# Moving part of a decoder layer's dense expert ahead of the routed experts, and its choice sums to other engines

## The chip, the cores and the metric

One core of a Trainium2 chip (trn2) runs the whole kernel in one launch. The metric is the device time of one execution in microseconds (us); lower is better. The engines of the core are TensorE (PE, with its weight loads as PEld), VectorE (DVE), ScalarE (ACT), GpSimd (POOL) and SyncE (SP)[...].

## The reference, cut to what matters

The kernel computes one decoder layer on x of 16 x 64 tokens by 256 columns, all in float32. Self-attention and cross-attention come first and are not touched. The last third is a mixture of experts on the normalized rows:

```python
scores = softmax(xt @ Wg.T)                # 1024 tokens, 16 experts
masked = scores where the expert's group is among the best 2 of 4 groups
topi = top_k(masked, 4)                    # 4 choices of each token
combine[t, topi] += scores[t, topi]
h = silu(xt @ W1[e].T) * (xt @ W3[e].T)    # each expert: 256 -> 176
y = sum over e of combine[:, e] * (h @ W2[e].T)
z = (silu(xt @ Ws1.T) * (xt @ Ws3.T)) @ Ws2.T     # shared expert, 352 wide
x = x + y + z
```

## The kernel before, in words

**Layout.** The 1024 tokens are 8 tiles of 128 rows, `x[0]` to `x[7]`; tiles 0 to 3 are half 0, 4 to 7 are half 1. A float32 product is made of two rounded parts, a high and a low one: ACT makes the high part (L112), DVE the low one (L113), and `three` (L107) multiplies high by high, high by low and low by high.

**The experts.** Experts 0 to 14 are computed on the rows that chose them only ("routed"). Expert 15, `w_last`, is computed densely, on all rows, and added with its weight, which is zero where it was not chosen (`add_last`, L933). The shared expert is dense too.

**Slots.** `choose` (L734) finds the four choices of each row and a place for each among 384 slots per expert. `send` (L820) writes rows to their slots in DRAM (`xd`) with indirect DMAs issued by POOL, four tiles for each choice and half. Of routed expert e, `expert_inputs` (L1233) loads the 384 rows on SP's queue once the sends of its possible choices have landed (expert 0 waits for first choices only, expert 1 for first and second, and so on), PE turns them (L1247), ACT and DVE make the parts `xs`. `expert_weights` loads 640 KB; ACT and DVE, later ACT, DVE and POOL, make the parts (L270, L275). `expert_hidden` (L1255) multiplies up (18 matmuls of 384 columns, `mm<-xs,w`) and gates. `send_outputs` (L1273) multiplies down (15 matmuls, `av<-w,hp`), copies to `y` (L1281) and writes the rows to the row's place in a second DRAM array, `yd`, with three indirect DMAs on POOL (L1286). `load_outputs(k)` (L1296) loads all choices number k back in four DMAs of 256 KB from SP's queue into `got` (nine buffers of two tiles for sixteen uses) once every send issued so far has landed. `add_outputs` (L1309) adds them with their weights `cw` (made by `weights_of_choices`, L852, one call for each half): for tiles 2 and 5 ACT scales (L1313) and POOL adds (L1314), for the other six one DVE instruction does both (L1316).

**Order.** The loop of L1335 runs over e: inputs of e, weights of e, hidden of e-1, outputs of e-2. For e = 2 alone, hidden of expert 1 is written ahead of the inputs of expert 2, and `issue_after(up_done[0])` puts the turning of expert 2's rows behind expert 1's up products on PE. A planner (`schedule_with_timeline_sim`, L1494) lays out each engine's queue: program order is the priority, and an instruction that its model takes to be ready may pass one that is not. `issue_after(ins)` only fixes an order on the engine of `ins`. On the chip each queue is then worked off in order, and an instruction that waits holds all behind it.

**Dense expert.** Half 0 is done ahead of the loop, beside the shared expert: `dense_up(0)` (L1069) with 512 columns at a time, `dense_gated`, `dense_out` (L1098). Half 1 is done in the last experts, 256 columns at a time: its first part's hidden at e = 16 (L1353), its output at L1368, its second part at L1370, between the additions of choices 0, 1 and of 2, 3.

**End.** L1364 puts the additions behind the last expert's instructions on each engine; each `x[i]` is then stored by SP or ACT's queue (L1374). An `If` (L1385) for slots that did not suffice ends the kernel; it is not entered here.

Of the kernel before, what the change touches and what calls it, by code (L numbers as in the profile page):

```python
# [35 lines left out]
NI = NT // 128  # L36
# [6 lines left out]
E, INTER, NGRP, TOPK, TOPKG = 16, 176, 4, 4, 2  # L43
# [28 lines left out]
def decoder_layer(ctx: ExitStack, tc: tile.TileContext, a: dict, out: bass.AP):  # L72
# [80 lines left out]
    norms, scaled, turned, silus, exps, softened = [], [], [], [], [], []  # L153
# [152 lines left out]
    with ExitStack() as attn:  # L306
# [545 lines left out]
        def weights_of_choices(half):  # L852


            shape = [128, 4, E]
            lg = logits[half]
            m = fs.tile([128, 4], F32, tag="r_m", name="r_m")
            nc.vector.tensor_reduce(m, lg, AX.X, ALU.max)
            p = fs.tile(shape, F32, tag=f"r_p{half}", name=f"r_p{half}")
            nc.vector.tensor_tensor(p, lg, m.unsqueeze(2).broadcast_to(shape), ALU.subtract)  # L860
            exps.append(nc.scalar.activation(p, p, AF.Exp).ins)
            s = fs.tile([128, 4], F32, tag="r_s", name="r_s")
            nc.vector.tensor_reduce(s, p, AX.X, ALU.add)
            nc.vector.reciprocal(s, s)
            nc.vector.tensor_tensor(p, p, s.unsqueeze(2).broadcast_to(shape), ALU.mult)
            sel = selected[half]
            last = fs.tile([128, 4], F32, tag=f"cl{half}", name=f"cl{half}")
            nc.vector.tensor_tensor(last, sel[:, :, E - 1], p[:, :, E - 1], ALU.mult)
            nth = fs.tile(shape, F32, tag="slot", name="nth_back")
            nc.vector.tensor_tensor(  # L870
                nth, places[half], sel[:, :, E - 1 :].broadcast_to(shape), ALU.add
            )
            ch = choices(nth, sel)
            kept = fs.tile(shape, F32, tag="slot", name="kept")
            nc.vector.scalar_tensor_tensor(kept, over[half], 0.5, p, ALU.is_lt, ALU.mult)
            nc.vector.tensor_tensor(
                ch, ch, kept.unsqueeze(1).broadcast_to([128, TOPK, 4, E]), ALU.mult
            )
            w = fs.tile([128, TOPK, 4], F32, tag=f"cw{half}", name=f"cw{half}")
            nc.vector.tensor_reduce(w, ch, AX.X, ALU.add)  # L880
            return w, last, p
# [57 lines left out]
        routed = []  # L939


        with (
# [143 lines left out]
            def dense_gated(g, up, g2, up2):  # L1086
                h_p = [
                    xa.tile([128, 512], F32R, tag=f"roped1{n}", name=f"dense1{n}", bufs=1)
                    for n in range(2)
                ]  # L1090
                h_p.append(xa.tile([128, 512], F32R, tag="q_r", name="dense2"))
                nc.vector.tensor_tensor(g, up, g, ALU.mult)
                parts_of(g, h_p[0], h_p[1])
                nc.vector.tensor_tensor(g2[:64], up2[64:], g2[64:], ALU.mult)
                parts_of(g2[:64], h_p[2][:64], h_p[2][64:])
                return h_p

            def dense_out(h_p, half, tiles, add):  # L1098
                for k in tiles:
                    ps = av_tile()[:, :D]  # L1100
                    expert_output(ps, w_last, h_p, slice(k * 128, k * 128 + 128))
                    add(half, k, ps)
# [9 lines left out]
            for n in range(len(units) + 2):  # L1112
# [58 lines left out]
                if n == 8:  # L1171
                    w_last = dense_weights()
                    with after(exps[-1]):
                        routed.append(weights_of_choices(0))
                if n == 9:
                    rows[1] = [
                        xw.tile([128, 3, 2, 2, DC], F32, tag="w_s", name="rows1")
                        .rearrange("p a b c d -> p (a b c d)")[:, : 2 * ROW]
                        .rearrange("p (a b) -> p a b", a=2)
                        for _ in range(2)  # L1180
                    ]
                    normed[1] = layernorm_t(3, (1,), token_rows(1))[0]
                    high = highs[-1]
                    scored, placed, aimed = choose(1)
                    sh = [
                        xb.tile([128, 2, 2, 4 * HQ], F32R, tag=f"w_q{m}", name=f"sh{m}")
                        .rearrange("p a b c -> p (a b c)")
                        for m in range(2)
                    ]
                    hs = []  # L1190
                    for k in range(3):
                        with after(*pn_turned[(0 if k else 1) :]):
                            up = shared_up(0, k, xa)
                            part = [t[:, k * 512 : (k + 1) * 512] for t in sh]
                            hs.append(shared_hidden(k, *up, xa, part))
                    send(0, (2,), [lows[-1]])
                    with after(projected, scaled[-1]):
                        shared_output(0, hs)
                    send(0, (3,), [high])
                    send(1)  # L1200
                    with after(high):
                        dense_ups = dense_up(0, turned[-1], scored, scored)
                    with after(aimed, scored):
                        ups = [shared_up(1, 0, xa)]
                    with after(aimed, placed):
                        ups.append(shared_up(1, 1, xa))
                        hs = [shared_hidden(k, *ups[k], xa) for k in range(2)]
                        ups.append(shared_up(1, 2, xa))
                        hs.append(shared_hidden(2, *ups[2], xa))
                        h_p = dense_gated(*dense_ups)  # L1210
                        shared_output(1, hs)
                        dense_out(h_p, 0, range(4), add_last)


    fw = ctx.enter_context(tc.tile_pool(name="fw", bufs=2, reuse_waits="tile"))
# [4 lines left out]
    gated, up_done = [None], [None]  # L1220
# [85 lines left out]
            tiles.append(t)  # L1306
        return tiles

    def add_outputs(k, got, cw):  # L1309
        for i in range(NI):  # L1310
            y, w = got[i // 2][:, i % 2], cw[i // 4][:, k, i % 4 : i % 4 + 1]
            if i % 3 == 2:
                nc.scalar.activation(y, y, AF.Copy, scale=w)  # L1313
                nc.gpsimd.tensor_tensor(x[i], x[i], y, ALU.add)  # L1314
            else:
                nc.vector.scalar_tensor_tensor(x[i], y, w, x[i], ALU.mult, ALU.add)  # L1316

    def dense_hidden(w, half, n):
        return expert_hidden(w, [p[:, :, n * 256 : n * 256 + 256] for p in normed[half]], 256)

    def dense_output(w, h_p, half, n, add):
        for b in range(2):
            ps = av_tile()[:, :D]
            expert_output(ps, w, h_p, slice(b * 128, b * 128 + 128))
            add(half, 2 * n + b, ps)
# [7 lines left out]
    with tc.issue_after(lows[-1]), tc.issue_after(silus[-1]):  # L1333
        ws[0] = expert_weights(a["W123"][0], nc.vector)
    for e in range(E + 1):  # L1335
        if e == 2:

            low = lows[-1]
            hs[e - 1] = expert_hidden(ws[e - 1], xs[e - 1][0], SLOTS)
        if e < E - 1:  # L1340
            low = lows[-1]
            with tc.issue_after(up_done[0] if e == 2 else low):
                xs[e] = expert_inputs(e)
            if e >= 1:
                with tc.issue_after(low), tc.issue_after(silus[-1]):
                    ws[e] = expert_weights(a["W123"][e], nc.vector if e < 3 else nc.gpsimd)
        if 0 <= e - 1 < E - 1 and e != 2:
            hs[e - 1] = expert_hidden(ws[e - 1], xs[e - 1][0], SLOTS)
        if e - 2 >= 0:
            if e == E:  # L1350

                with tc.issue_after(gated[0]):
                    h_p = dense_hidden(w_last, 1, 0)  # L1353
            last = send_outputs(e - 2, ws.pop(e - 2), hs.pop(e - 2), xs.pop(e - 2)[1])
            if e - 2 == E - TOPK - 2:
                short = slots_are_short()
            if e == 6:
                with tc.issue_after(gated[0]), tc.issue_after(silus[-1]):
                    routed.append(weights_of_choices(1))
            k = e - 2 - (E - 1 - TOPK)  # L1360
            if k >= 0:
                got[k] = load_outputs(k)
    with ExitStack() as behind_last:
        for ins in (*last, gated[0]):  # L1364
            behind_last.enter_context(tc.issue_after(ins))
        cw = [r[0] for r in routed]
        add_outputs(0, got[0], cw)
        dense_output(w_last, h_p, 1, 0, add_last)  # L1368
        add_outputs(1, got[1], cw)
        dense_output(w_last, dense_hidden(w_last, 1, 1), 1, 1, add_last)  # L1370
        for k in range(2, TOPK):
            add_outputs(k, got[k], cw)
    for i in range(NI):
        (nc.sync if i % 2 == 0 else nc.scalar).dma_start(  # L1374
            out=out[i * 128 : (i + 1) * 128, :], in_=x[i]
# [122 lines left out]
```

## Time and profile before

| | us |
|---|---|
| median of 3 runs (lowest, highest) | 592.65 (592.43, 593.28) |
| profiled execution, own time | 594.01 |
| its span, first to last instruction | 592.2 |

| engine | busy us | share of the span |
|---|---|---|
| PE | 558.4 | 94% |
| DVE | 403.4 | 68% |
| ACT | 280.6 | 47% |
| POOL | 232.5 | 39% |

Three stretches of the trace concern the change. From 446 to 460 us the shared expert's and the dense expert's first half run on PE while POOL sends rows; from 460 to 475 the first two routed experts start; from 560 to 592 the last experts end, and the choices are loaded, added and stored. The mean granted clock of PE over the span is 0.973 of full speed. A row of the timeline has the start, the duration of the merged instructions, engine, line, operation, written and read tile, shape and number of instructions, then the idle time ahead of it and what ended that. A busy time of merged matmuls is their stretch; a mean duration of one (300 to 400 ns) is longer than its share of that stretch (190 ns), since matmuls overlap.

### The profile page before, as it was taken

To read this page: it belongs to the slowest core of one execution; us is meant where nothing else is said; L and a number is where in the kernel's file an instruction comes from. 1 tells how busy PE (TensorE), PEld (TensorE's weight loads), DVE (VectorE), ACT (ScalarE), POOL (GpSimd) and SP (SyncE) were. 2 spreads that over 40 slices of the span, in tenths; PEclk is the share of its full clock that TensorE was granted. 3 is DMA by queue.
4 is the path that set the end of the run, shared out by engine and by line. 5 is a ranking of instruction groups with operands and counts; after the bars stand their busy time and mean duration, and the time that the engine had idled before them with its cause. 6 is when DMAs were issued, how large, how long until landed. Compare 5 with 4: busy or idle time off the path is not lost.

```text
span 592.2 us, 10572 instructions
## 1 busy us (share of the span) xinstructions
PE 558.4 (94%) x3999; PEld 452.9 (76%) x3999; DVE 403.4 (68%) x879; ACT 280.6 (47%) x524; POOL 232.5 (39%) x213
## 2 busy tenths in 40 slices
PE   5989999999999989999999999999989799999992
PEld 5878988988889875757777577576778688888871
DVE  5454636554465789847668487789648587888766
ACT  3657574575665432221431332333435276867551
POOL 4192000010000004526334454442545546768773
PEclk8989999999999999999999999999989799999996
DMA  8667042141300499481020000000413677565275
GB/s 247 159 195 208 25 136 91 53 143 50 95 1 1 137 265 293 128 243 30 1 70 1 8 1 1 28 2 26 165 69 95 231 225 239 176 228 184 100 252 184
DMA packets 56293, 70.82 MB, mean 120 GB/s; under 512 B 13872, under 2 KB 42768, under 8 KB 56240
## 3 DMA queue, kind: packets, MB, share of 16 engines
q1 hardware_dynamic: 51408, 58.71, 33.5%
q0 software_dynamic: 3696, 10.36, 4.6%
q10 hardware_dynamic: 1136, 1.05, 0.5%
q8 instruction: 32, 0.52, 0.4%
q14 instruction: 21, 0.17, 0.1%
HBM read 48.61 MB, written 21.86 MB: 119 GB/s over the span
## 4 chain that ended last, share of the span: by engine, by line


## 5 line engine op out<-in xcount | busy, mean ns | idle before, releaser
L973 POOL TENSOR_TENSOR roped<-rt,rt 128x512 f32<-128x512 f32 x48 | 62.7, 1328 | 82.8 <-DVE rt L967 80.5
L967 DVE TENSOR_TENSOR rt<-mm,rope_q 128x512 f32<-128x512 f32 x96 | 61.5, 684 | 23.7 <-PE mm L104 23.1
L104 PE MATMUL mm<-xn,w_q 128*128 128x512 f32 x288 | 74.2, 403 | 0.5 <-ACT xn L214 0.5
L104 PEld LDWEIGHTS mm<-xn,w_q 128*128 128x128 f32 x288 | 52.1, 188 | 14.4 <-issue 2.7
L1286 POOL DMA_INDIRECT yd<-y,to x45 | 49.4, 1099 | 34.7 <-DVE y L1281 13.5
L104 PE MATMUL mm<-xs,w 128*128 128x384 f32 x270 | 57.0, 358 | 1.2 <-ACT w L270 0.6
L104 PEld LDWEIGHTS mm<-xs,w 128*128 128x128 f32 x270 | 48.0, 196 | 4.4 <-DVE w L275 0.8
L318 ACT ACTIVATE p<-p 128x512 f32<-128x512 f32 x32 | 20.2, 630 | 65.7 <-DVE p L317 65.7
L513 POOL TENSOR_TENSOR wo<-code,scale 128x512 fp32r<-128x512 f32 x8 | 10.6, 1330 | 102.1 <-PE mm L104 94.1
L988 PE MATMUL mm<-roped,w_s 128*64 128x512 f32 x192 | 46.3, 601 | 0.0
L104 PE MATMUL av<-w,hp 128*128 128x256 f32 (+1 forms) x225 | 45.8, 314 | 0.1
L605 DVE TENSOR_TENSOR x<-mm,x 128x256 f32<-128x256 f32 x64 | 26.0, 419 | 29.1 <-PE mm L104 27.9
L104 PEld LDWEIGHTS av<-w,hp 128*128 128x128 f32 (+1 forms) x225 | 33.9, 187 | 9.0 <-issue 0.7
L104 PE MATMUL mm<-wo,o 128*128 128x256 f32 x256 | 39.5, 295 | 0.1
L104 PE MATMUL mm<-wv,xn 128*128 128x256 f32 x256 | 36.0, 292 | 1.4 <-ACT kT L550 1.4
L315 DVE TENSOR_REDUCE sm_m<-at 128x8 f32<-128x512 f32 x32 | 21.7, 679 | 21.8 <-PE at L565 20.9
L104 PE MATMUL mm<-xn,wq 128*128 128x512 f32 x128 | 35.4, 413 | 0.4 <-ACT xn L214 0.4
L104 PE MATMUL mm<-xn,wk 128*128 128x512 f32 x128 | 35.4, 407 | 0.0
L582 PE MATMUL av<-pt,v 128*128 128x128 f32 x256 | 34.5, 277 | 0.0
L104 PEld LDWEIGHTS mm<-wv,xn 128*128 128x128 f32 x256 | 32.5, 193 | 2.5 <-ACT kT L550 1.6
L104 PEld LDWEIGHTS mm<-wo,o 128*128 128x128 f32 x256 | 32.9, 190 | 1.5 <-issue 0.4
L582 PEld LDWEIGHTS av<-pt,v 128*128 128x128 f32 x256 | 32.0, 191 | 1.2
(216 smaller groups left out, 1150.1 us busy)
## 6 DMA issues: line engine op xcount, KB each, us to landing
w<-in_W SPq DMA_DIRECT2D x15, 640.0 KB
code<-in_codes SPq DMA_DIRECT2D x32, 256.0 KB
scale<-in_scales SPq DMA_DIRECT2D x32, 256.0 KB
xr<-xd SPq DMA_DIRECT2D x15, 408.0 KB
xd<-zeros SPq DMA_DIRECT2D x8, 720.0 KB
yd<-zeros SPq DMA_DIRECT2D x8, 512.0 KB
got<-yd SPq DMA_DIRECT2D x16, 256.0 KB
wq<-in_Wq SPq DMA_DIRECT2D x4, 512.0 KB
```

Source lines behind the costliest of these rows:

```text
L104: m = nc.tensor.matmul(ps, lhsT=l, rhs=r, start=(n == 0), stop=(n == len(pairs) - 1))
L315: nc.vector.tensor_reduce(m, sc, AX.X, ALU.max)
L318: exps.append(nc.scalar.activation(p, p, AF.Exp, scale=scale).ins)
L513: mults[n] = eng.tensor_tensor(w, *loaded[gr].pop(n), ALU.mult).ins
L582: nc.tensor.matmul(av[:, k * 128 : (k + 1) * 128], lhsT=v[:, i, k0 : k0 + HD], rhs=pt[:, i].rearrange("p a q -> p (a q)"), start=True, sto ...
L605: nc.vector.tensor_tensor(x[i], ps, x[i], ALU.add)
L967: nc.vector.tensor_tensor(mt, ps3, rope_table(t, 2 * ab + k), ALU.mult)
L973: nc.gpsimd.tensor_tensor(r.rearrange("p (b s) -> p b s", s=S), one, two, op)
L988: nc.tensor.matmul(ps[h // 2][(h % 2) * 64 : (h % 2) * 64 + 64], lhsT=w_s[:, t, blk, ab, :], rhs=roped[2 * t + ab], start=first[h], stop=l ...
L1286: sent = nc.gpsimd.indirect_dma_start(out=yd[: (E - 1) * SLOTS + min(TOPK, E - 1 - e) * NT], out_offset=bass.IndirectOffsetOnAxis(ap=to[:, ...
```

## The change

Three edits.

1. For e = 1 as well as e = 2, hidden of expert e-1 is written ahead of the inputs of e, and expert 1's turning goes behind expert 0's up products on PE. Since `silus[-1]` is then expert 0's, the parts of expert 1's weights go behind expert 0's gate on ACT.
2. The dense expert's half 1 leaves the last experts and is done whole ahead of the loop, 512 columns at a time, after half 0's output; the weights of the choices of half 1 are made there too, no longer at e = 6.
3. Choice 0 is added wholly by ACT (scale) and POOL (add), in three portions in iterations e = 14, 15 and 16, each written behind that iteration's three sends of rows and ahead of the next load of choices. Choices 1 to 3 are added at the end, tiles 1, 4 and 7 by ACT and POOL, five tiles by DVE.

```diff
                         dense_out(h_p, 0, range(4), add_last)
+                        routed.append(weights_of_choices(1))
+                        h_p = dense_gated(*dense_up(1, placed, placed, placed))
+                        dense_out(h_p, 1, range(4), add_last)
...
-    def add_outputs(k, got, cw):
-        for i in range(NI):
-            y, w = got[i // 2][:, i % 2], cw[i // 4][:, k, i % 4 : i % 4 + 1]
-            if i % 3 == 2:
+    def add_outputs(k, got, tiles=range(NI), others=(1, 4, 7)):
+        for i in tiles:
+            y, w = got[i // 2][:, i % 2], routed[i // 4][0][:, k, i % 4 : i % 4 + 1]
+            if i in others:
                 nc.scalar.activation(y, y, AF.Copy, scale=w)
                 nc.gpsimd.tensor_tensor(x[i], x[i], y, ALU.add)
...
-        if e == 2:
+        if e in (1, 2):
             low = lows[-1]
             hs[e - 1] = expert_hidden(ws[e - 1], xs[e - 1][0], SLOTS)
         if e < E - 1:
             low = lows[-1]
-            with tc.issue_after(up_done[0] if e == 2 else low):
+            with tc.issue_after(up_done[0] if e in (1, 2) else low):
                 xs[e] = expert_inputs(e)
...
-        if 0 <= e - 1 < E - 1 and e != 2:
+        if 0 <= e - 1 < E - 1 and e > 2:
             hs[e - 1] = expert_hidden(ws[e - 1], xs[e - 1][0], SLOTS)
         if e - 2 >= 0:
-            if e == E:
-                with tc.issue_after(gated[0]):
-                    h_p = dense_hidden(w_last, 1, 0)
             last = send_outputs(e - 2, ws.pop(e - 2), hs.pop(e - 2), xs.pop(e - 2)[1])
...
-            if e == 6:
-                with tc.issue_after(gated[0]), tc.issue_after(silus[-1]):
-                    routed.append(weights_of_choices(1))
             k = e - 2 - (E - 1 - TOPK)
+            if k >= 1:
+                tiles = ((), (0, 1, 2), (3, 4, 5), (6, 7))[k]
+                add_outputs(0, got[0], tiles, tiles)
             if k >= 0:
                 got[k] = load_outputs(k)
...
-        cw = [r[0] for r in routed]
-        add_outputs(0, got[0], cw)
-        dense_output(w_last, h_p, 1, 0, add_last)
-        add_outputs(1, got[1], cw)
-        dense_output(w_last, dense_hidden(w_last, 1, 1), 1, 1, add_last)
-        for k in range(2, TOPK):
-            add_outputs(k, got[k], cw)
+        for k in range(1, TOPK):
+            add_outputs(k, got[k])
```

## The prediction, made before the changed kernel was run

> **What bounds the kernel now.** I read the busy times by stretch first, to see which engine rules where the change works.
>
> ```profile
> 446.00:460.00 14.00, 14.00 (x84) 11.55 (x84) 11.51 (x23) 7.49 (x12) 9.51 (x9) 1.00 0.33 100
> 460.00:475.00 15.00, 10.67 (x49) 10.05 (x48) 7.63 (x17) 4.74 (x10) 8.08 (x8) 0.77 0.71 232
> 475.00:560.00 85.00, 83.89 (x485) 72.59 (x484) 70.58 (x131) 59.51 (x118) 57.39 (x48) 1.00 0.61 198
> 560.00:572.00 12.00, 12.00 (x72) 10.20 (x71) 7.08 (x13) 5.63 (x15) 8.52 (x8) 1.00 0.56 187
> 572.00:592.00 20.00, 7.71 (x39) 5.61 (x38) 15.01 (x31) 5.26 (x13) 9.52 (x11) 0.72 0.66 218
> ```
>
> The columns are stretch, length, busy PE, PEld, DVE, ACT, POOL, then PE's clock. PE is the bound in every stretch but 460 to 475, where it idles and its clock falls to 0.77, and the last 20 us, where DVE is busy 15. So a moved PE instruction costs its full time unless it falls into one of these two.
>
> Next, the timeline of PE where the routed experts start: expert 0's up products have begun, then PE stands still for expert 1's rows, with 15 of expert 0's 18 products queued behind the turning.
>
> ```profile
> 459.57 0.82 PE L1247 MATMUL at<-ident,xr 128*128 128x128 f32 x6
> 460.63 0.79 PE L104 MATMUL mm<-xs,w 128*128 128x384 f32 x3 [0.24 <-ACT xs L112]
> 465.50 0.87 PE L1247 MATMUL at<-ident,xr 128*128 128x128 f32 x3 [4.09 <-DMA xr<-xd]
> 466.03 3.23 PE L104 MATMUL mm<-xs,w 128*128 128x384 f32 x9
> 469.05 0.84 PE L1247 MATMUL at<-ident,xr 128*128 128x128 f32 x3
> 469.55 5.32 PE L104 MATMUL mm<-xs,w 128*128 128x384 f32 x24
> ```
>
> The gap is 4.09 us, and nine matmuls after it take 3.23 us, 0.36 each, where 18 take 3.41 later (0.19 each, at 540.13).
>
> Last, the end, as DVE and POOL see it.
>
> ```profile
> 571.47 5.00 DVE L1316 SCALAR_TENSOR_TENSOR x<-got,cw,x 128x256 f32<-128x256 f32 x10
> ...
> 585.54 1.66 DVE L1316 SCALAR_TENSOR_TENSOR x<-got,cw,x 128x256 f32<-128x256 f32 x4
> ```
>
> ```profile
> 561.98 1.11 POOL L1286 DMA_INDIRECT yd<-y,to  x1 [0.16 <-issue]
> ...
> 572.58 1.00 POOL L1286 DMA_INDIRECT yd<-y,to  x1 [0.30 <-ACT y L1281]
> 573.88 1.28 POOL L1286 DMA_INDIRECT yd<-y,to  x1 [0.30 <-ACT got L1313]
> 575.18 2.74 POOL L1314 TENSOR_TENSOR x<-x,got 128x256 f32<-128x256 f32 x3
> 578.98 2.46 POOL L1314 TENSOR_TENSOR x<-x,got 128x256 f32<-128x256 f32 x3 [1.06 <-ACT got L1313]
> 583.12 1.83 POOL L1314 TENSOR_TENSOR x<-x,got 128x256 f32<-128x256 f32 x2 [1.67 <-ACT got L1313]
> ```
>
> DVE works from 571.47 to 587.2 without a gap that the timeline marks: 24 additions (12.6 us) and the dense half's own gating and adding. It sets the end; the last store closes the span 5.0 us later. POOL issues its nine last sends one after the other from 561.98 to 575.16 and has only eight additions.
>
> [...] 0.36 us a matmul for 3.2 us after the gap, then 0.22, then 0.19. [...] POOL's additions take 725 to 1002 ns (median 902) beside a full DVE, while the same shape took 740 in the median at L634. [...] the send ending at 453.17 lets SP's load go at 455.20.
>
> **The change, step by step: the start.** Moving half 1 ahead adds PE work before the routed experts: 18 up products of 512 columns at 0.243 us (24 took 5.82 from 445.80), 4.4 us, and 20 down products at 0.191 (20 took 3.83 from 568.33), 3.8 us: +8.2. What they can hide in: the gaps of 4.09 and 0.24, which close because PE has work until about 468 while expert 1's rows land at 465.5: -4.3. Without the gap the clock stays up: from 465.50 to 474.87 PE does 33 up products and 6 turnings in 9.4 us, which at 0.189 and 0.137 would be 7.1: -2.3. Balance +1.6. Edit 1 closes the same gap, so it is worth nothing beside edit 2 (alone it would fill 15 x 0.19 = 2.9 us of it); what it costs is a wait: the ACT part of expert 1's weights (1.26) now stands behind expert 0's gate, with DVE's low part (0.95) behind that and expert 1's products behind both. Dense half 1's down products, 3.8 us, are there to cover its 2.2.
>
> New stalls: unknown. DVE gets from the move 2 gate products, 2 low parts (0.69 each), 4 additions (0.48) and the choices' weights (some 3.1 for thirteen small ones): 7.8 us on top of the 9.7 that it has from 450.94 until expert 0's rows are done. That is 17.6, filled until 468.5 at best, against PE's 468: no bound, but no slack. ACT gets 3.5 of gating and casts and two table loads (1.28 each). Between 0, if the planner's order always finds PE something ready, and 3.0, if the two chains take turns; a gain is excluded, as only idle PE time counted above can be won. The nearest row is half 0's own down products, 16 in 3.43 (0.214 against 0.191), 0.4 us lost. I take 1.0 for both products and weights.
>
> The weights of half 1's choices leave e = 6, where the table loads held ACT and PE waited 0.58 us for expert weights (at 512.32): -0.6. POOL's sends of rows and SP's loads keep their order there. So the routed experts run **2.0 us later** (1.6 + 1.0 - 0.6).
>
> **The end, in the clock of before.** PE loses 18 of the dense products (2.57 us of 561.19 and 566.80) between the last experts, so the last down product could end 2.3 to 2.6 us before 572.1; DVE goes from 24 additions to 15 and has nothing dense: some 8 us of work. What is next is POOL. From 561.98 on (it makes the last expert's low weights until 561.82, gated by ACT's cast, which PE does not advance) it has nine sends at 1.27 us from start to start (0.96 and 0.30 of issue), 11.4, and now 8 + 3 x 3 = 17 additions instead of 8. Their price: 0.725 at the least, 0.95 beside a full DVE; DVE is some 40% busy there, and I take 0.82: 13.9. With 0.4 for hand-overs POOL ends at 561.98 + 11.4 + 13.9 + 0.4 = **587.7**, against DVE's 587.2 before. The order among them does not matter: with the additions ahead, the last send ends at about 578.4, the last rows' load starts 2.4 later and is in by 586.4 (four loads, 5.6 us, estimated from got's second-last set: issue 574.30, second load in at 578.34), and the last scale and addition end at 588; with the sends ahead, 13 to 14 additions still follow 576. ACT's scales are covered by POOL's. In both the stores take the same 5.0 us. The end costs **+0.5**.
>
> Sum: 592.2 + 2.0 + 0.5 = 594.7 of span, and as the median lies 0.45 above that span, 592.65 + 2.5 = **595.1**. (The profiled execution itself took 594.01, 1.8 above its span; I carry only the difference over.)
>
> **Rivals.**
> - *The early stretch hides the moved half (not slower).* Place: PE from 446 to 475. PE is called full there, but down products at 0.214 and the stall behind DVE's additions show slack; if dense half 1 fills these too and brings no new stall, +2.0 becomes +0.2, giving 593.3; it decides once new stalls are under 0.4 us. Against it: DVE's 17.6 us.
> - *POOL is not the last.* Additions at 0.725 (-1.6), and the last store alone in the DMA queues in 4.0 instead of 5.0 us: 592.5. For it: DVE is relieved. [...] With the first rival also true, 590.7.
> - *In-order queues wait on each other (slower).* ACT's scale of choice 0 sits among the last expert's gates and waits for a DMA, POOL's addition waits for ACT, and sends stand behind it; and the two early chains take turns (3.0): +2.0 and +2.2 at the end, 599.3.
> - *The edit of the order does nothing of its own*: the time is the forecast's, since the gap is counted once.
>
> **How the numbers follow.** Forecast, 0.48, own range 593.9 to 597.2 (stalls 0 to 2, additions 0.78 to 0.88). First rival 0.16, second 0.11, both together 0.10, queues 0.15. About 1.2 us (0.2%) is what this kernel's measurement can tell. Below 591.4: both rivals together and part of each, 0.21. From 591.4 to 593.9: the rest of these, 0.2. Above: 0.59. The range runs from 590.5 (both first rivals, rounded down) to 599.3 (the queues' case; stalls of 3.0 and additions at 0.95, +2.0 and +2.2, give the same), which leaves out about 0.1 at the lower end and 0.06 at the upper.
>
> **What would show it.** PE has no gap over 1 us from 446 to 476 and its clock stays at 1.0; expert 1's up products end at 477.5; POOL is busy from expert 12's sends to within 1 us of the last addition; DVE idles in the last 15 us. Wrong if the last additions are DVE's, if POOL idles over 3 us there, or if the experts start no later than before.

## The result and the profile after

| | before | after |
|---|---|---|
| median (lowest, highest), us | 592.96 (592.43, 595.69), 4 runs | 613.37 (611.10, 614.44), 4 runs |
| ratio (95% interval) | | 1.033 (1.0286 to 1.0373) |
| profiled execution, own time and span | 594.01, 592.2 | 611.10, 609.0 |

The change makes the kernel 3.3% slower. The sign of the forecast was right; the size was not: 613.4 lies far above the range that ended at 599.3. The profiled execution is the fastest of the four, so the traces account for 16.8 us of the 20.4 between the medians. (Of the last two kernels of the table below 7 of 14 and 8 of 22 executions are slow, over 602 us, at a mean granted clock of 0.961 to 0.971 where the others have 0.969 to 0.985, against 1 of 35 of before beside them; they are in the median and left out of the ratio, and what slows them is not shown.)

To say where they went I cut each trace at two matmuls whose place no edit changes: the last of `placed` (L781), just ahead of the work that the change touches, and the one of `slots_are_short` (L838), when the outputs of expert 10 have been sent. What lies ahead of the first mark is the same program in every kernel here, yet its end falls anywhere from 441.7 to 450.0 us, so only stretches are compared, not clock times. Each stretch is of one profiled execution. Where kernels have the same program in a stretch, they differ by up to 1.5 us (117.6 to 119.1 in four of the table below, 40.7 to 42.1 at the end of six), so less than that is not read as an effect.

| stretch | before | after | difference |
|---|---|---|---|
| start to L781 | 445.6 | 442.8 | -2.8 |
| L781 to L838 | 105.8 | 119.0 | **+13.2** |
| L838 to the end | 40.8 | 47.2 | **+6.4** |

So the routed experts run 13.2 us later where 2.0 was forecast, and the end costs 6.4 where 0.5 was forecast.

First the busy times of after by stretch, with the columns of the prediction's first block (stretch, length, then busy PE, PEld, DVE, ACT, POOL, PE's clock, DMA share, GB/s).

```profile
457.00:472.00 15.00, 10.75 (x38) 7.42 (x36) 7.03 (x13) 5.83 (x8) 7.58 (x8) 0.80 0.53 182
...
590.00:609.00 19.00, 0.00 (x0) 0.00 (x0) 7.75 (x10) 3.05 (x6) 7.28 (x10) 0.50 0.53 171
```

The first row should have been full: in before a hole of 4 us stood there, for rows from DRAM, and the moved products were to fill it. It is as empty as before (10.75 busy of 15), and its clock is low (0.80). The last 19 us have no PE work at all.

The timeline of PE in after, where dense half 1 now stands:

```profile
456.69 4.46 PE L104 MATMUL mm<-xn,w_last 128*128 128x512 f32 x18
463.13 1.30 PE L104 MATMUL av<-w_last,dense 128*128 128x256 f32 x6 [1.97 <-ACT dense L112]
466.66 5.43 PE L104 MATMUL av<-w_last,dense 128*128 128x256 f32 x14 [2.22 <-DVE dense L113]
472.02 1.54 PE L1250 MATMUL at<-ident,xr 128*128 128x128 f32 x6
473.49 4.64 PE L104 MATMUL mm<-xs,w 128*128 128x384 f32 x18
...
480.42 0.79 PE L104 MATMUL mm<-xs,w 128*128 128x384 f32 x3 [1.64 <-ACT xs L112]
...
482.23 1.84 PE L104 MATMUL mm<-xs,w 128*128 128x384 f32 x9 [0.54 <-DVE xs L113]
```

The planner has put the shared expert and half 0 first, and the whole of half 1 after them. Between its up products and its down products PE's queue holds nothing else, so PE stands still while ACT and DVE make the gate: 1.97 us, six matmuls, 2.22 us. The 14 that follow take 5.43 us, 0.39 each against 0.19. From 456.69 to expert 0's turning at 472.02 half 1 has taken **15.3 us**; its products alone are the 8.2 of the prediction. ACT's side of that chain shows what it is made of:

```profile
458.44 1.28 ACT L1080 ACT_TABLE_LOAD   x1 [6.40 <-PE mm L104]
...
462.46 0.62 ACT L112 CAST dense<-dense 128x512 fp32r<-128x512 f32 x1
462.98 1.26 ACT L270 CAST w<-w 128x1280 fp32r<-128x1280 f32 x1
464.15 0.61 ACT L112 CAST dense<-dense 64x512 fp32r<-64x512 f32 x1
```

ACT and DVE are far from full here (5.83 and 7.03 of the 15 us). What counts is their latency, the time from a step's start to its end while PE waits for it: on ACT a table load of 1.28, four steps of 0.6, the two casts, and expert 0's weights (1.26) between these.

The end, POOL in after:

```profile
576.11 3.15 POOL L1317 TENSOR_TENSOR x<-x,got 128x256 f32<-128x256 f32 x4
579.42 0.98 POOL L1289 DMA_INDIRECT yd<-y,to  x1 [0.16 <-issue]
...
589.33 0.96 POOL L1289 DMA_INDIRECT yd<-y,to  x1 [0.31 <-issue]
590.31 4.90 POOL L1317 TENSOR_TENSOR x<-x,got 128x256 f32<-128x256 f32 x6
```

These are additions of choice 0 (four of the eight), a send behind them, the last send, and additions of the later choices. All eight of choice 0 stand ahead of the last four sends, and POOL works from 572.44 to 590.29 with no pause but the sends' own 0.3 us. The last send ends 28.5 us after L838; in before it was 23.8. Choice 3's rows are in about 9.8 us after that send (ACT's last scale starts at 600.19, released by them), and DVE, which has little else now, waits for the rows of the choices:

```profile
590.97 4.51 DVE L1319 SCALAR_TENSOR_TENSOR x<-got,cw,x 128x256 f32<-128x256 f32 x5 [4.95 <-DMA got<-yd]
```

Last, the close. POOL's queue ends with a record that the prediction overlooked. In before (count, then shortest, median and longest in ns, then the first and last start):

```profile
L1494 POOLq DRAIN  x3: 40/107/6355, 585.1 to 592.0; - x3
```

And in after:

```profile
L1489 POOLq DRAIN  x3: 40/107/6355, 601.8 to 608.7; - x3
```

The long DRAIN starts 0.2 us after POOL's last addition (584.95 and 601.55) and takes 6.36 us. The span ends 7.3 and 7.4 us after that addition. So even in before it was POOL that closed the kernel, though not by much: SP's own DRAIN, behind its stores, stands at 590.0, and POOL's long one is over at 591.5. That DVE's last addition, at 587.2, lay 5.0 us before the end was chance.

### The profile page after: what moved, and what is told of

Its sections match the earlier page's. It is cut to its first block, busy times and chain, and to the rows that moved or that the text cites. A ratio compares the mean times of both kernels' runs of the same rounds, so it can differ in the third digit from the quotient of the medians.

```text
span 609.0 us, 10538 instructions
## 1 busy us (share of the span) xinstructions
PE 561.1 (92%) x3981; PEld 454.2 (75%) x3981; DVE 399.6 (66%) x866; ACT 284.3 (47%) x531; POOL 236.0 (39%) x222
## 5 line engine op out<-in xcount | busy, mean ns | idle before, releaser
L967 DVE TENSOR_TENSOR rt<-mm,rope_q 128x512 f32<-128x512 f32 x96 | 61.4, 683 | 23.7 <-PE mm L104 23.1
L1289 POOL DMA_INDIRECT yd<-y,to x45 | 46.5, 1032 | 50.9 <-ACT y L1284 25.1
L104 PE MATMUL av<-w,hp 128*128 128x256 f32 (+1 forms) x225 | 48.3, 326 | 2.2 <-ACT y L1284 2.2
L104 PEld LDWEIGHTS av<-w,hp 128*128 128x128 f32 (+1 forms) x225 | 35.5, 196 | 11.3 <-ACT y L1284 3.2
```

The costliest lines, as they stand in the source:

```text
L104: m = nc.tensor.matmul(ps, lhsT=l, rhs=r, start=(n == 0), stop=(n == len(pairs) - 1))
L967: nc.vector.tensor_tensor(mt, ps3, rope_table(t, 2 * ab + k), ALU.mult)
L1289: sent = nc.gpsimd.indirect_dma_start(out=yd[: (E - 1) * SLOTS + min(TOPK, E - 1 - e) * NT], out_offset=bass.IndirectOffsetOnAxis(ap=to[:, ...
```

## The experiments

The stretches of every kernel, in us (L781 to L838, and from there to the end). Each ratio is to before on the same chip, where before's median was 593.0 to 594.4, so medians of two rows from different chips can be 1 to 2 us apart for that alone. The interval of after overlaps with those of the three runs that change one thing in it (the rows "after, ..."): there only the traces tell them apart. The traces of edit 2 alone and of the dense half in the gap are of the slowest execution of their kernel.

| kernel | L781 to L838 | L838 to end | median | ratio (95%) |
|---|---|---|---|---|
| before | 105.8 | 40.8 | | |
| after | 119.0 | 47.2 | 613.37 | 1.033 (1.029-1.037) |
| edit 1 alone | 104.6 | 41.7 | 592.83 | 0.998 (0.996-1.000) |
| edit 2 alone | 121.3 | 40.7 | 610.33 | 1.024 (1.018-1.029) |
| edit 3 alone | 105.4 | 47.8 | 601.74 | 1.013 (1.008-1.019) |
| edits 1 and 2 | 117.6 | 41.1 | 606.26 | 1.019 (1.015-1.024) |
| after, expert 0's weights ahead | 116.2 | 47.7 | 610.58 | 1.027 (1.024-1.031) |
| edits 1, 2, half 1 pipelined | 119.2 | 42.1 | 608.83 | 1.021 (1.015-1.027) |
| edits 1, 2, chain cut | 109.5 | 41.6 | 598.18 | 1.008 (1.005-1.010) |
| edit 2, chain cut | 106.0 | 41.4 | 594.02 | 1.000 (0.998-1.003) |
| edit 1, expert 1's weights first | 108.4 | 41.0 | 597.27 | 1.006 (1.003-1.008) |
| dense half in the gap | 112.3 | 41.4 | 598.59 | 1.008 (1.005-1.012) |
| after, last choices on DVE | 119.1 | 43.5 | 610.65 | 1.028 (1.024-1.032) |
| after, choice 0 behind the sends | 117.7 | 46.4 | 610.92 | 1.028 (1.024-1.032) |
| edit 1, dense part behind | 104.3 | 41.0 | 601.10 | 0.999 (0.995-1.003) |
| edit 1, one addition to DVE | 104.8 | 40.8 | 597.75 | 1.001 (0.999-1.004) |

**Which edit costs what.** Edits 1 and 2 without edit 3 (the additions as before):

```diff
-    def add_outputs(k, got, tiles=range(NI), others=(1, 4, 7)):
+    def add_outputs(k, got, tiles=range(NI), others=(2, 5)):
...
-            if k >= 1:
-                tiles = ((), (0, 1, 2), (3, 4, 5), (6, 7))[k]
-                add_outputs(0, got[0], tiles, tiles)
...
-        for k in range(1, TOPK):
+        for k in range(TOPK):
             add_outputs(k, got[k])
```

> Edits 1 and 2 stay, edit 3 is undone: all four choices are added at the end, tiles 2 and 5 by ACT and POOL, the others by DVE. Theory (ACT's scales of choice 0 stand among the last experts' gates and POOL's additions among their sends; that costs some 5 us on the last send, and 2 to 3 more at the end): with the dense half gone from the end the last send comes about 2.5 us earlier than in the kernel before after taking off the early loss of 10.4, and the time is about 600. Rival (the end is lost because all loss is inherited from the early stretch, edit 3 being neutral): 611 to 614, as the changed kernel.

606.26, 7.1 below after, and the stretch to the end is 41.1: the loss at the end is gone, the early one stays, and the time lies between the theory's 600 and the rival's 611. Edit 3 alone, on before (its three hunks of the diff, the dense half left at the end):

> The kernel before with edit 3 alone: choice 0 by ACT and POOL in the last experts, tiles 1, 4, 7 of the other choices too; the dense second half stays in the last experts. Theory (ACT's scales hold the last gates, POOL's additions hold the last sends): the last send 4 to 5 us later, time 597 to 600. Rival (DVE was the bound of the end and is relieved of 9 additions, 4.7 us): 588 to 591.

601.74, a little above the theory's range, and the stretch to the end is 47.8, 7.0 more than before: the loss at the end is edit 3's. This run shows how the queues hold each other. ACT, then POOL, when choice 0's rows come:

```profile
565.90 0.91 ACT L1313 ACTIVATE got<-got,cw 128x256 f32<-128x256 f32 x2 [3.81 <-DMA got<-yd]
566.72 0.74 ACT L1265 ACTIVATE g<-mm 128x384 f32<-128x384 f32 x2
```

```profile
567.14 4.17 POOL L1314 TENSOR_TENSOR x<-x,got 128x256 f32<-128x256 f32 x6
571.48 1.12 POOL L1286 DMA_INDIRECT yd<-y,to  x1 [0.16 <-ACT got L1313]
```

ACT's queue waits 3.81 us for a load, with an expert's gate behind it; then POOL adds for 4.17 us while a send of rows stands behind. And edit 2 takes nothing off the end: 41.1 with half 1 gone from there, 40.8 with it. PE and DVE have less to do, and neither was what closed the kernel.

Edit 1 alone, on before:

```diff
-        if e == 2:
+        if e in (1, 2):
...
-            with tc.issue_after(up_done[0] if e == 2 else low):
+            with tc.issue_after(up_done[0] if e in (1, 2) else low):
...
-        if 0 <= e - 1 < E - 1 and e != 2:
+        if 0 <= e - 1 < E - 1 and e > 2:
```

> The kernel before with edit 1 alone: expert 0's up products ahead of expert 1's turning. Theory (the gap of 4.1 us is filled by 15 products, the slow clock after it mostly goes): 2.5 to 4.5 us faster, about 589. Rival (the wait that edit 1 brings, expert 1's weights behind expert 0's gate on ACT, takes the place of the gap; PE stands 2 us for them and the rows of expert 1 are the limit anyway): within 1 us of the kernel before.

592.83, ratio 0.998 (0.996 to 1.000), and 1.2 us less in the stretch, which is less than two traces can tell. The 4.09 us gap is gone, and other waits have most of its place:

```profile
465.66 0.79 PE L104 MATMUL mm<-xs,w 128*128 128x384 f32 x3 [1.58 <-ACT xs L112]
...
467.46 3.12 PE L104 MATMUL mm<-xs,w 128*128 128x384 f32 x9 [0.54 <-DVE xs L113]
```

ACT's part of expert 1's rows is late, as it stands behind the cast of expert 1's weights, which edit 1 has put behind expert 0's gate. Edit 2 alone (edits 1 and 3 undone):

> Edit 2 alone, edits 1 and 3 undone: the dense half ahead, expert 1's weights and turning ordered as before the change. Prediction's step (edit 1 is worth nothing beside edit 2): the time of edits 1 and 2 together, 605 to 607.5. Theory W (edit 1 makes the cast of expert 1's weights wait behind expert 0's gate, and the dense half's products no longer cover it, since all of them are done by then; the waits of 1.64, 0.54, 0.52 and 0.27 add up to 3.0): 602 to 604.5. Rival G (a gap for expert 1's rows is still there and edit 1 fills it): above 607.5.

610.33. By the ratios (1.024 against 1.019, with overlapping intervals) it can't be told from edits 1 and 2 together, but theory W's 602 to 604.5 is missed. The trace gives two answers. From expert 0's turning to L838 it takes 85.1 us against 88.4 with edit 1: there, edit 1 costs 3.3. But dense half 1 took 7.0 us more: ACT's first Silu comes 4.6 us after its products begin, where in after it comes 1.75 us after them, and then ACT stands 2.3 and 0.9 and PE 1.2 us with no releaser in the trace. I can't say what held them; the trace is of an execution 3.5 us above this kernel's median, so part of it may be that execution's own. Cutting the chain, below, goes round it.

**The early stretch.** After, with the parts of expert 0's weights ordered behind what lay ahead of half 1:

```diff
+                        ahead = lows[-1], silus[-1]
                         routed.append(weights_of_choices(1))
                         h_p = dense_gated(*dense_up(1, placed, placed, placed))
...
-    with tc.issue_after(lows[-1]), tc.issue_after(silus[-1]):
+    with tc.issue_after(ahead[0]), tc.issue_after(ahead[1]):
         ws[0] = expert_weights(a["W123"][0], nc.vector)
```

> The changed kernel, but expert 0's weights are ordered behind the shared expert's last Silu, as in the kernel before, and no longer behind the dense second half's Silu. Theory A (that order wait is the early loss: it holds expert 0's low weights, behind them on SP's queue expert 2's weights and behind those expert 0's rows): expert 0's rows are loaded by 456 instead of 466.5, the first turning comes near 463 instead of 472, and the time falls by 8 to 10 us to about 604. Rival B (the dense second half's own chain from PE over ACT and DVE back to PE is the loss, because nothing else stands in PE's queue to cover it; the rows landed as the queue reached them): only the 1.6 us of DVE work that stood in that chain is won, and some of the slow clock: 1.5 to 4 us, about 610.

610.58, rival B's figure; the stretch is 2.8 us shorter, no more. Expert 0's rows now come early: their load is issued 13.1 us after L781, where in after it stands on SP's queue behind a load of weights that waits for its buffer, and goes at 23.7. PE's wait for DVE falls from 2.22 to 0.22, and the first wait of 1.97 and the slow clock stay:

```profile
462.51 1.30 PE L104 MATMUL av<-w_last,dense 128*128 128x256 f32 x6 [1.97 <-ACT dense L112]
464.03 5.28 PE L104 MATMUL av<-w_last,dense 128*128 128x256 f32 x14 [0.22 <-DVE dense L113]
```

So most of the loss is half 1's own chain, not the rows.

Edits 1 and 2, with half 1's steps written between those of half 0 and the shared expert:

```diff
                         h_p = dense_gated(*dense_ups)
-                        shared_output(1, hs)
+                        dense_ups = dense_up(1, placed, placed, placed)
                         dense_out(h_p, 0, range(4), add_last)
                         routed.append(weights_of_choices(1))
-                        h_p = dense_gated(*dense_up(1, placed, placed, placed))
+                        h_p = dense_gated(*dense_ups)
+                        shared_output(1, hs)
                         dense_out(h_p, 1, range(4), add_last)
```

> Edits 1 and 2 without edit 3, and dense half 1's up products written ahead of half 0's down products, its gate ahead of the shared expert's down products, its own down products behind those; the same instructions in another order. Theory B (the moved half took 15.3 us and not 8.2 because PE had nothing else in its queue between the steps of that half's chain): the 4.2 us of idle time and most of the 2.9 us of slow clock go, 606.3 becomes 599 to 601. Rival (the stall belongs to DVE and ACT, which are too full for the moved half wherever it stands, as when it stood in the gap at expert 1: it comes back as waits of the first experts): 604 to 607.

608.83: the rival's number, or worse. But the stall is not where the rival puts it; it stays in half 1:

```profile
467.60 0.80 PE L104 MATMUL av<-w_last,dense 128*128 128x256 f32 x2 [3.51 <-ACT dense L112]
468.90 6.45 PE L104 MATMUL av<-w_last,dense 128*128 128x256 f32 x18 [0.51 <-issue]
```

Both halves share the same tiles for the gated rows, so half 1's high part can't be written until PE has read half 0's (its last products end at 463.19), and ACT makes it only at 466.93, with no releaser shown for the rest. So this order doesn't take the chain away, and the run decides nothing.

So the chain was taken away with PE's work left in place: half 1's up products are made and nothing waits for them (the kernel leaves out half 1's gate, so its sums are not the layer's).

```diff
-                        h_p = dense_gated(*dense_up(1, placed, placed, placed))
+                        dense_up(1, placed, placed, placed)
                         dense_out(h_p, 1, range(4), add_last)
```

> Edits 1 and 2 without edit 3, with the chain of dense half 1 cut: its up products and their copies are made, but its gate and the two parts of it are left out, and its down products read half 0's gated rows, which are there long before. PE does the same matmuls, and waits for nothing in that half. Theory B (half 1 took 15.3 us instead of 8.2 because PE stood at each step of its chain, and the clock fell with it): 5 to 7 less than edits 1 and 2 together, 599 to 601.5. Rival (PE would stand there in any case, for the rows of expert 0, which land late): 604 or more.

> The same cut chain, and edit 1 undone as well: edit 2 without its chain, and the first experts in the order of before. Prediction's step (edit 1 is worth nothing beside edit 2): within 1 us of the cut chain with edit 1. Theory W (edit 1 adds waits for the parts of expert 1's rows and weights that nothing covers, 3.0): 2 to 3.5 less than with edit 1. Rival G (PE now comes to expert 1's rows before they land, and edit 1 fills that gap): 1 to 4 more.

With edit 1, 598.18: 8.1 us less than edits 1 and 2 together, in the stretch and in the median alike (6.9 by the two ratios to before), where theory B had 5 to 7. The same matmuls now run like this:

```profile
462.52 4.47 PE L104 MATMUL mm<-xn,w_last 128*128 128x512 f32 x18
466.82 2.90 PE L104 MATMUL av<-w_last,dense 128*128 128x256 f32 x15
469.66 0.88 PE L1250 MATMUL at<-ident,xr 128*128 128x128 f32 x6
...
477.34 0.79 PE L104 MATMUL mm<-xs,w 128*128 128x384 f32 x3 [1.58 <-ACT xs L112]
```

There is no gap in half 1 and no slow stretch (its 15 down products in 2.90 us are 0.19 each), and edit 1's waits (1.58 here, then 0.54) are still there. Without edit 1, 594.02: 4.2 less again, 3.5 in the stretch, a little more than theory W's 2 to 3.5. Its timeline has the products of experts 0 and 1 with two short waits, the longer of 0.74:

```profile
469.46 0.80 PE L104 MATMUL mm<-xs,w 128*128 128x384 f32 x3 [0.74 <-ACT xs L112]
...
472.65 4.48 PE L104 MATMUL mm<-xs,w 128*128 128x384 f32 x24
```

The cut has two side effects. It takes 2.7 us of DVE work and two casts away, and without half 1's low parts expert 0's rows are loaded earlier, 9.5 us after L781 instead of 23.7. So this pair alone doesn't exclude its rival, that PE would have stood for late rows. The run with expert 0's weights ahead does: there the rows are early too and the chain stands, and its stretch of 116.2 is 6.7 above the 109.5 of the cut chain. Half 1's chain thus costs 6.7 of the 8.1 us; the rest is the rows or the scatter between traces. Once the chain is gone, edit 1 costs 3.5, and the moved products without either cost 0.3 in the stretch and nothing that the times can tell (ratio 1.000, 0.998 to 1.003).

Two runs tried other places. Edit 1 on before, with expert 1's weights written ahead of expert 0's hidden:

```diff
+        if e == 1:
+            with tc.issue_after(lows[-1]), tc.issue_after(silus[-1]):
+                ws[e] = expert_weights(a["W123"][e], nc.vector)
         if e in (1, 2):
...
-            if e >= 1:
+            if e >= 2:
```

> Edit 1 alone on the kernel before, but expert 1's weights are written ahead of expert 0's hidden part, so that ACT makes their high part before expert 0's gate, as in the kernel before. Theory (what edit 1 wins by filling the gap is given back by the wait for expert 1's rows' parts, which stand behind expert 1's weights on ACT and DVE): the waits of 1.58 and 0.54 us on PE after the second turning go, 1.5 to 3 us faster than edit 1 alone, about 590 beside 592.8. Rival (the rows of expert 1 and the chain turning, parts, products are the limit in any order): no change against edit 1 alone.

597.27, slower than edit 1 alone: missed. The wait of 1.58 for ACT is gone, but expert 2's rows come later: their load is issued 26.3 us after L781 (22.3 with edit 1 alone), and PE waits 4.31 us for them. The trace puts SP's wait ahead of this load down to the sends of rows, which must land first (the last 4.3 us of it). A second load of weights, 640 KB, now goes out 18.4 us after L781, among these sends, where with edit 1 alone it goes after 27.6. Whether it is this load that holds the sends up is not shown. On top of this, dense half 1, 256 columns at a time, into the gap (its steps in the last experts and the call for its weights at e = 6 are taken out):

```diff
             hs[e - 1] = expert_hidden(ws[e - 1], xs[e - 1][0], SLOTS)
+            if e == 1:
+                first = up_done[0]
+                routed.append(weights_of_choices(1))
+                dense_expert(w_last, 1, add_last)
+                up_done[0] = first
```

> The dense second half is moved ahead as in edit 2, but into the loop, behind expert 0's up products, 256 columns at a time with the routed experts' buffers; expert 1's weights ahead of expert 0's hidden part; additions at the end as in the kernel before (edit 3 undone). Theory (the dense half cost 15 us instead of 8 because nothing else stood in PE's queue while its chain went over ACT and DVE; with expert 0's and 1's turnings and products between its steps it costs what its matmuls take, and the gap takes most of it): early stretch within 2 us of the kernel before, end some 2 us shorter, time 588 to 593. Rival (8 us of matmuls ahead of the routed experts delay them by that wherever they stand): 597 to 600.

598.59, within the rival's range. The same late load is in it (26.2 us after L781), so it can't say whether half 1 fits there; that stays open. It does confirm that the end gains nothing (41.4).

**The end.** After, with choices 2 and 3 added by DVE alone:

```diff
     def add_outputs(k, got, tiles=range(NI), others=(1, 4, 7)):
+        if k >= 2:
+            others = ()
```

> The changed kernel, with choices 2 and 3 added by DVE alone, so that POOL's last addition is one of choice 1. Theory D (the span ends 7.3 us after POOL's last instruction, of which a record of 6.36 us on POOL's queue is a fixed part; DVE's last addition costs 5 us): POOL ends 8 us earlier, DVE's last addition near 601.3 in the changed kernel's clock, and the time falls by 2 to 3 us. Rival (the end is the last rows' landing, the store and its completion, whichever engine adds): no change, or up to 1 us slower since DVE has six more additions.

610.65, 2.7 below after, as theory D had it; the stretch to the end is 3.7 shorter. POOL ends at 593.74 and DVE at 602.58:

```profile
L1491 POOLq DRAIN  x3: 40/107/6355, 593.9 to 606.8; - x3
L1491 SPq DRAIN  x3: 7/7/7, 606.2 to 606.5; - x3
```

The long DRAIN is over at 600.3, long before the end; now SP's own DRAIN, behind its stores, comes last, at 606.2, and the span ends at 607.0. In after SP's stood at 604.9 and the span went on to 609.0, waiting for POOL. Choice 0 by ACT and POOL, but behind the last sends:

```diff
-            if k >= 1:
-                tiles = ((), (0, 1, 2), (3, 4, 5), (6, 7))[k]
-                add_outputs(0, got[0], tiles, tiles)
...
+        add_outputs(0, got[0], range(NI), range(NI))
         for k in range(1, TOPK):
             add_outputs(k, got[k])
```

> The changed kernel, with choice 0's additions on the same engines (ACT, POOL), but written at the end, behind the last sends. Theory (POOL's work is the bound: nine sends and eight additions one after the other set the last send; behind it stand a load of rows and nine more additions): the last send is 5 to 6 us earlier, POOL's seventeen additions follow it, and the time falls by 1 to 3 us, since POOL still ends last. Rival (only the place of the additions among the sends costs, POOL has time enough): 5 to 6 us faster.

610.92. The last send ends 22.4 us after L838, 6.1 sooner than in after, and POOL ends only 0.9 sooner (38.8 against 39.7 after L838), for the seventeen additions are still to come: 15 of them in 11.76 us without a pause. So the theory held: the order moves the time from one place to another, and the work on POOL is what it costs.

**A better version?** Edit 1 alone with the dense half's first part behind the last expert's down products, and choice 3 of tile 5 added by DVE; and edit 1 with the second of these only:

```diff
-            if e == E:
-                with tc.issue_after(gated[0]):
-                    h_p = dense_hidden(w_last, 1, 0)
...
+        h_p = dense_hidden(w_last, 1, 0)
         cw = [r[0] for r in routed]
         add_outputs(0, got[0], cw)
...
-            if i % 3 == 2:
+            if i == 2 or (i == 5 and k < 3):
```

> Edit 1 alone, with the dense half's first part in the last experts put behind the last expert's down products, and one addition of POOL's (choice 3 of tile 5) given to DVE. Theory (POOL's last sends wait for PE: 18 dense products, 0.87 and 1.70 us, stand ahead of the last two experts' products, and POOL idles 1.52 and 0.27 us for these): the last send ends up to 1.8 us earlier, 590.5 to 592.0 against 592.8 of edit 1 alone. Rival (the dense half's own chain then ends last): 593.5 or more.

> Edit 1 alone, with choice 3 of tile 5 added by DVE and not by ScalarE and POOL. Theory D (the span ends 7.3 us after POOL's last instruction, 583.24 + 7.3 = 590.5 in edit 1 alone, where DVE's last addition at 584.71 and the stores would let it end at 589.1 to 589.7): POOL ends 0.9 earlier, DVE 0.45 later, 0.3 to 0.8 less than edit 1 alone, 592.0 to 592.5. Rival (DVE and the stores set the end): 0.4 more, 593.2.

Ratios 0.999 (0.995 to 1.003) and 1.001 (0.999 to 1.004): neither can be told from before. In both the span ends 8.3 and 8.9 us after POOL's last instruction, so POOL no longer closes the kernel, and still nothing is won: the stores end only 3.7 and 4.6 us after DVE's last addition. Edit 1 alone, at 0.998, has the lowest ratio, at the edge of what can be told.

## Why the prediction was wrong

**What bounds the kernel: half right.** PE in every stretch but the two named, yes. "DVE sets the end; the last store closes the span 5.0 us later" was wrong: POOL's last addition and its DRAIN did. The prediction took DVE's for the last step because it ends later and never followed POOL's queue past its last busy instruction.

**The balance of PE's work: right.** 8.2 of products, less 4.3 of gap and 2.3 of slow clock, less 0.6 for the weights of the choices, is +1.0. Where the chain is cut and edit 1 undone, the stretch is 0.3 longer; the forecast and this differ by less than two traces can tell.

**"New stalls: I take 1.0", bounded by 0 and 3.0: the step that failed.** The prediction compared sums of work, DVE filled until 468.5 against PE until 468, and called it "no bound, but no slack". What decides is latency: half 1's four steps run one after another, PE has nothing else queued between them, and the sum of the engines' work says nothing of it. Half 1 took 15.3, 7.1 over its products; the upper bound of 3.0 came from no row of the trace: half 0's chain was seen only with the shared expert's products between its steps. That "each queue is then worked off in order" stood in the description of the kernel, and the trace of before shows it of PE (15 of expert 0's products stand 4.09 us behind a turning); it was not applied to half 1's products.

**"Edit 1 is worth nothing beside edit 2": wrong.** It costs 3.5 us where the chain is cut. Its wait was priced at 2.2 and the dense half's down products "are there to cover" it; in after these are all done by 472.02, ahead of expert 0's turning, and the waits (1.64, 0.54, 0.52, 0.27) are bare. The rest of the missing credit is the slow clock that half 1's gaps leave behind: expert 0's six turnings and 18 up products take 1.54 and 4.64 us, where those at full clock take 0.82 and 3.41, 1.9 more. From expert 0's turning to L838 the prediction credited 7.2 us (4.3, 2.3 and 0.6); the stretch got 2.0 shorter (89.8 against 91.8). The missing 5.2 are about the sum of the two, 3.5 and 1.9. These 5.2 and the 7.1, less the 1.0 allowed, are the 11.2 us between 2.0 and 13.2 (to rounding).

**The end: POOL as the bound was right, and so was the price of its additions; its wait for the last rows was left out.** Seventeen additions at 0.82 were to take 13.9 us and take 13.95. That DVE's load is what moves them between 0.725 and 0.95 was the author's estimate and is not shown: in after, six from 590.31 on take 0.82 each with DVE busy 4.23 of 4.89 us. But in the clock of before (10.4 us off) POOL ends at 591.1, not 587.7, for it waits 4.2 us in all for the last choices. With the additions ahead, which happened, the last send was to end at 578.4, which fits six of the eight additions ahead of it; the planner put all eight there, and it ends at 579.9. The rows were to be in 8.0 us later and take 9.8. Then "the stores take the same 5.0 us", where POOL's close takes 7.4. Together 3.4 + 2.5 = 5.9, the difference between +0.5 and +6.4. "The order among them does not matter" was nearly right: 0.9 us at POOL's end.

**The rivals.** "In-order queues wait on each other" named what happened, in both places, and priced it at a third: it has 6.7 us where 20.4 were lost. "The early stretch hides the moved half" would have come true for the products alone (+0.3). "POOL is not the last" fell (its 4.0 us for the last store was an estimate; in the last two kernels of the table the stores end 3.7 and 4.6 us after DVE's last addition), and so did "the edit of the order does nothing of its own" (3.5 us with the chain cut).

**What would show it.** PE was to have no gap over 1 us early on; it has two in half 1 (1.97 and 2.22) and one of 1.64 behind expert 1's turning. Its clock was to stay at 1.0; it is 0.80 from 457 to 472. Expert 1's up products end at 485.4, which is 488.2 in the clock of before, not 477.5. POOL is busy from the sends on until 595.2, then waits for rows, 4.2 us in three waits, which is over the 3 us that the prediction named as a sign of being wrong. DVE idles in the last 15 us, as said (4.95 and 1.27).

What stays open: what held ACT for 2 to 4 us in half 1 in two of the runs; whether half 1 would pay in the gap without the early load of weights; and whether, with tiles of its own for its gated rows, its chain could run beside half 0.

## What to carry to other kernels

When work is moved to where an engine has a hole, its products fill the hole only if its whole chain does (half 1 took 15.3 us for 8.2 of products): write down, step by step, what each engine has queued between the steps, and add the latencies where it has nothing. And before work is taken off an engine at the end, find what closes the kernel, down to the last record of each queue: relief elsewhere buys nothing (edit 2, nothing at the end: 40.7 us against 40.8), and additions given to the closing engine are paid in full (edit 3: nine more at 0.82 are 7.4, and the end got 7.0 longer).

## What the runs showed of the hardware

- None of the sixteen kernels ends earlier than 7.29 us after POOL's last instruction. In thirteen it is 7.29 to 7.58. In before, after and the run with the last choices on DVE, POOL's queue then has one DRAIN of 6.36 us. In the other three (the last choices on DVE and the last two of the table) POOL's last instruction lies 8.3 to 13.3 us ahead of the end, and the end comes 3.7 to 4.6 us after DVE's last addition.
- In after, PE's clock stayed at 1.00 through the first of two gaps (1.97 and 2.22 us with six matmuls between), fell to 0.50 during the second, and stayed there until about 476.2, 9.5 us after PE had resumed at 466.66 to be busy without a pause. In before it was 1.00 until 464, in the gap of 4.09 us, 0.83 in the us after, then 0.50 from PE's start at 465.50 through 470 to 471 and 0.75 in the us after: some 6 us of work. What sets these times is not shown. After, clock in the last column but two:

```profile
467.00:469.00 2.00, 2.00 (x5) 1.16 (x5) 0.68 (x2) 0.00 (x0) 0.00 (x0) 0.50 0.89 299
...
473.00:475.00 2.00, 2.00 (x8) 1.67 (x7) 1.19 (x3) 0.92 (x2) 0.00 (x0) 0.50 0.01 2
475.00:477.00 2.00, 2.00 (x10) 2.00 (x9) 0.00 (x0) 0.00 (x0) 0.00 (x0) 0.71 0.44 121
```
